# Emitting the scale of a feed-forward matrix later, and letting a reused buffer wait tile by tile

## The chip, the cores and the metric

The kernel runs on one core of a Trainium2 chip. The metric is the device time of one execution in microseconds (us); a lower one is better. Engines are called as in the profile: PE is TensorE, DVE is VectorE, ACT is ScalarE, POOL is GpSimd, SP is SyncE (which only issues transfers here).

## What is computed

A gated cross-attention block followed by a gated feed-forward block, over 16 batches of 224 tokens with 512 features. The context has 750 keys per batch, of which a mask leaves out some.

```python
x = x + tanh(g_xattn) * xattn(layernorm(x), ctx, mask, W_q, W_k, W_v, W_o, b_o)   # 8 heads of 64
x = x + tanh(g_ffn)   * ffn(layernorm(x), w1, b1, w2, b2)                        # 512 -> 2048 -> 512

def bitlinear(x, w, b):
    xq = act_quant(rmsnorm(x))          # rows to 8-bit integers and back
    scale = 1.0 / clip(mean(abs(w)), 1e-5)
    wq = clip(round(w * scale), -1, 1) / scale
    return einsum("bsd,fd->bsf", xq, wq) + b

def ffn(x, w1, b1, w2, b2):
    return bitlinear(gelu(bitlinear(x, w1, b1)), w2, b2)
```

What matters here is `scale`: it needs the mean of all absolute values of a weight matrix, so no weight can be rounded to -1, 0 or 1 before the whole matrix has been read and summed.

## The kernel before

The work goes batch by batch. The batches are sorted by how many keys the mask leaves, and only those keys are gathered: up to 192 for the first eight batches, up to 128 for the others. A sorted batch is called a slot. The loop at the end of `compact_path` runs over the 16 slots. In slot s it mixes three streams of pieces, each piece a small function with an estimated cost:

- `attention_pieces(s)`: the attention of slot s. It has empty pieces called wait, which only stand for time; `turn_probs` for the units 0 and 1 (a unit is four heads of half the tokens); the scores of units 2 and 3 (`both(2)`); `turn_probs` 2 and 3; and `weighted`, the sum over the values. `turn_probs` transposes the probabilities on PE (L1128, L1135). `scores` makes matmuls (L1074), reductions on DVE (L1088), exponentials on ACT (L1098), and a division on POOL (L1108), which `turn_probs` needs.
- `other`: what the next slots need. Norm of x (L979 to L988), gathers (L807, L880), `select(s + 3)` with six indicators on DVE (L830), then, woven together, `context_pieces(s + 1)` (transposes L905, keys L916, values L931 and L942) and `query_pieces(s + 1)` (transposes L1014, queries L1035).
- `flow`: in slot 0 the first feed-forward matrix (`weight_pieces(0)`), in slot 1 the second (`weight_pieces(1)`), from slot 2 on the output projection and the feed-forward block itself (`residual`, `project`, `normalise`, `up`, `gelu`, `down`).

`merge` takes, again and again, the next piece of the stream that is least far in terms of its own total cost; at equal shares the stream named first. After the streams come the scores of units 0 and 1 of slot s + 1. The order in which pieces are emitted is a priority: the Tile scheduler takes, for each engine, the ready instruction with the highest priority by its own model of time, and the queue that results is fixed. On the chip every engine then works through its queue in order.

A feed-forward matrix is handled in 8 chunks of 128 x 1024 values. `load_weights` reads a chunk into a `raw` tile; the chunks of the second matrix are loaded into the same 8 tiles as those of the first come free in slot 0. `sum_weights` sums absolute values (DVE L1388, ACT L1392). `scale_weights` adds up the sums (DVE L1398), sums over partitions with a matmul by ones (PE L1400) and takes reciprocals (DVE L1402 to L1411). `round_weights` multiplies and clips a chunk (DVE L1421, L1422), with three buffers for the result. `turn_weights` transposes it in eight matmuls (PE L1437 for the second matrix) and copies the result to `w2T` (an eviction, by DVE at L777 or ACT at L780). `evict` chooses the engine by two running counters of estimated work, to which other steps, `round_weights` among them, add too. The cost of a round is 0.2, of a turn 0.6, so the stream of a matrix has the total 8 x 0.8 = 6.4, and `scale_weights(1)` costs 0.

`w2T` is first read in `down` (PE L1329).

The raw tiles lie in a pool of their own, opened in `late["stage"]`. When slot 1 has been emitted, that pool is closed and the pool `rows` is opened on the memory: three `y` tiles of 4 KB per partition, three `hq` (which hold the rows of `gelu` and, in `normalise`, `fx`) and two `hqT`, 32 KB as the eight raw tiles. `residual` fetches the rows of `y` with POOL (L807) and adds the bias (L1207); `project` adds the projection (PE L1214, DVE L1217).

Of the kernel before, what the change touches and what calls it, by code (L numbers as in the profile page):

```python
# [733 lines left out]
def compact_path(ctx, tc, sh, x, context, out, late_loads, stages):  # L734
# [47 lines left out]
    def gen(shape, dtype, name):  # L782
        return ps_gen.tile(shape, dtype, tag="gen", name=name)
# [12 lines left out]
    def small(name, n=2):  # L796
        return pa.tile([P, n], F32, tag=f"s{n}", name=name, bufs=24 if n == 2 else 6)
# [73 lines left out]
    def gather(s):  # L871
        st = live[s]
        nt = 2 if CAPS[s] > P else 1
        if s:
            kept = pa.tile([P, 2, C], F32, tag="ctx", name=f"ctx_{s}", bufs=2)
        else:
            kept = early[:, 2 * D : 2 * D + 2 * C].rearrange("p (t c) -> p t c", t=2)
        for t in range(nt):
            rows = rows_of(s, t)
            nc.gpsimd.indirect_dma_start(  # L880
                out=kept[:rows, t, :],
                out_offset=None,
                in_=kctx,
                in_offset=bass.IndirectOffsetOnAxis(ap=st["keys"][:rows, t : t + 1], axis=0),
                bounds_check=B * J - 1,
                oob_is_err=False,
            )
        st["ctx"] = kept
# [163 lines left out]
    def norm_pieces(s):  # L1052
        pieces = []
        for t in tiles_of(s):
            if t % 2 == 0:
                pieces.append((0.0, lambda t=t: norm(t // 2)))
                if t // 2 + 2 < NTOK // 2:
                    pieces.append((0.0, lambda t=t: fetch(t // 2 + 2)))
        return pieces
# [138 lines left out]
    late = {}  # L1198

    def residual(i):  # L1200

        f = pairs[i] = {}
        f["y"] = y = late["rows"].tile([P, 2, D], F32, tag="y", name=f"y_{i}", bufs=3)
        for k in range(2):
            fetch_x(y[:, k, :], 2 * i + k)
        for k in range(2):
            nc.gpsimd.tensor_tensor(y[:, k, :], y[:, k, :], sh.bo, ALU.add)  # L1207
# [138 lines left out]
    def up_pieces(i):  # L1346
        p = []
        for k in range(2):
            p += [(1.8, lambda g=g, k=k: up(i, k, g)) for g in range(2)]
            p.append((0.0, lambda k=k: gelu(i, (k,))))  # L1350
        return p
# [15 lines left out]
    def load_weights(wi, c):  # L1367

        raws[wi, c] = raw = late["raw"].tile([P, W], F32, tag="raw", name=f"raw_{wi}_{c}", bufs=NPC)
        if wi == 0 and c == 0:  # L1370

            nc.scalar.copy(raw[0:1, 0:1], live[0]["ctx"][0:1, 0, 0:1])
        if wi == 0:
            return nc.sync.dma_start(
                raw.rearrange("p (a d) -> p a d", d=D),
                sh.w1_dram[c * 2 * P : (c + 1) * 2 * P, :].rearrange("(a p) d -> p a d", p=P),
            ).ins
        at = c % 2 * W
        return nc.sync.dma_start(raw, sh.w2_dram[c // 2 * P : (c // 2 + 1) * P, at : at + W]).ins

    def sum_weights(wi, c):
        if c == 0:
            weight_sums.append(pa.tile([P, NPC], F32, name=f"wsums_{wi}"))
        if c == 1:
            late["junk"] = pa.tile([P, FF], F32, tag="h", name=f"junk_{wi}", bufs=2)
        raw = raws[wi, c]
        if c % (2 + 2 * wi) == 0:
            nc.vector.tensor_reduce(  # L1388
                weight_sums[wi][:, c : c + 1], raw, AX.X, ALU.add, apply_absolute_value=True
            )  # L1390
        else:
            nc.scalar.activation(late["junk"][:, :W], raw, AF.Abs, accum_out=weight_sums[wi][:, c : c + 1])  # L1392
# [3 lines left out]
    def scale_weights(wi):  # L1396
        tot = small(f"wtot_{wi}")
        nc.vector.tensor_reduce(tot[:, 0:1], weight_sums[wi], AX.X, ALU.add)  # L1398
        pt = gen([P, 1], F32, f"wtotp_{wi}")
        nc.tensor.matmul(pt, lhsT=sh.ones, rhs=tot[:, 0:1], start=True, stop=True)  # L1400
        mean = small(f"wmean_{wi}")
        nc.vector.tensor_scalar(mean[:, 0:1], pt, 1.0 / (FF * D), 1e-5, ALU.mult, ALU.max)  # L1402
        sw = pa.tile([P, 1], F32, name=f"sw_{wi}")
        nc.vector.reciprocal(sw, mean[:, 0:1])
        isw = pa.tile([P, 1], F32, name=f"isw_{wi}")
        nc.vector.reciprocal(isw, sw)
        if wi == 0:
            nc.vector.tensor_scalar(isw, isw, 1.0 / 127.0, None, ALU.mult)
        else:

            nc.vector.tensor_scalar(isw, isw, sh.tgates[:, 1:2], 1.0 / 127.0, ALU.mult, ALU.mult)  # L1411
        weight_scale[wi] = sw
        sh.isw[wi] = isw
# [3 lines left out]
    def round_weights(wi, c):  # L1417

        raw = raws.pop((wi, c))
        quantised[wi, c] = w16 = pa.tile([P, W], BF16, tag="xq", name=f"w16_{wi}_{c}", bufs=3)  # L1420
        nc.vector.tensor_scalar(raw.bitcast(I32), raw, weight_scale[wi], None, ALU.mult)  # L1421
        nc.vector.tensor_scalar(w16, raw.bitcast(I32), 1.0, -1.0, ALU.min, ALU.max)  # L1422
        load["v"] += 1400

    def turn_weights(wi, c):
        w16 = quantised.pop((wi, c))
        pt = gen([P, 8, P], BF16, f"wp_{wi}_{c}")
        if wi == 0:

            for d in range(ND):  # L1430
                for a in range(2):
                    at = a * D + d * P
                    nc.tensor.transpose(pt[:, 2 * d + a, :], w16[:, at : at + P], ident16)
            evict(w1T[:, :, c * 2 * P : (c + 1) * 2 * P], pt.rearrange("p (d a) f -> p d (a f)", d=ND), 8 * P)
        else:
            for f in range(8):
                nc.tensor.transpose(pt[:, f, :], w16[:, f * P : (f + 1) * P], ident16)  # L1437
            f = c % 2 * 8
            evict(w2T[:, f : f + 8, c // 2 * P : (c // 2 + 1) * P], pt, 8 * P)

    def weight_pieces(wi):

        p = []
        if wi == 1:
            p += [(0.0, lambda: scale_weights(1))]
        for c in range(NPC + 2):
            if c < NPC:
                p += [(0.2, lambda c=c: round_weights(wi, c))]
                if wi == 0:
                    p += [(0.0, lambda c=c: load_weights(1, c))]  # L1450
            if c > 1:
                p += [(0.6, lambda c=c: turn_weights(wi, c - 2))]
                if wi == 0:
                    p += [(0.0, lambda c=c: sum_weights(1, c - 2))]
        return p
# [18 lines left out]
    def weave(a, b):  # L1474

        outl = []
        ia = ib = 0
        while ia < len(a) or ib < len(b):
            if ib >= len(b) or (ia < len(a) and ia * len(b) <= ib * len(a)):
                outl.append(a[ia])  # L1480
                ia += 1
            else:
                outl.append(b[ib])
                ib += 1
        return outl
# [11 lines left out]
    ctx = stages[0]  # L1497
# [40 lines left out]
    for s in range(B):  # L1538
        other = norm_pieces(s + 2) if s + 2 < B else []
        if s + 2 < B:  # L1540
            other.append((0.0, lambda s=s: gather(s + 2)))
        if s + 3 < B:
            other.append((0.0, lambda s=s: select(s + 3)))
        if s + 1 < B:
            other += weave(context_pieces(s + 1), query_pieces(s + 1))
        flow = []
        if s < 2:
            flow = weight_pieces(s)
        else:
            complete = 256 * (projected + 1) <= S * s  # L1550
            if projected == 0:
                nc.gpsimd.tensor_scalar(sh.bo, sh.bo, sh.tgates[:, 0:1], None, ALU.mult)
                nc.gpsimd.tensor_scalar(sh.b2, sh.b2, sh.tgates[:, 1:2], None, ALU.mult)
            if complete:
                flow.append((0.0, lambda i=projected: residual(i)))
            if raised < projected:
                flow += up_pieces(raised)
                raised += 1
            if complete:
                flow += project_pieces(projected)  # L1560
                projected += 1
                if lowered < raised:
                    flow += down_pieces(lowered)
                    lowered += 1
        merge(attention_pieces(s), other, flow)
        if s == 1:

            late["stage"].close()
            late["rows"] = ctx.enter_context(tc.tile_pool(name="rows", bufs=1))
        if s + 1 < B:  # L1570
            scores(s + 1, 0)
            scores(s + 1, 1)
# [45 lines left out]
```

## Time and profile before

| | us |
|---|---|
| median of 3 runs | 751.12 |
| lowest, highest | 750.07, 753.04 |
| the profiled execution | 751.76 |
| its span in the profile | 750.0 |
| PE busy | 681.3 |
| DVE busy | 499.0 |
| ACT busy | 408.0 |
| POOL busy | 394.1 |

The span runs from the first to the last instruction in the profile; the time of the execution has 1.76 us more around it. A line of the timeline gives the start and the duration in us, the engine, the source line, the operation, the tiles (written <- read), the shape and the number of instructions merged; in brackets stands the idle time before it, and what ended that. A line of the windows gives for each engine the busy time and the number of instructions, then the clock that PE was granted (1.00 is full speed) and the share and rate of the DMA engines.

### The profile page before, as it was taken

How to read it: one execution, taken by the hardware profiler on the slowest of the kernel's cores; microseconds unless marked ns; L12 is line 12 of the kernel's file. 1: busy time of each engine (PE TensorE's matmuls, PEld its weight loads, DVE VectorE, ACT ScalarE, POOL GpSimd, SP SyncE). 2: the span in 40 equal slices, each digit the busy share in tenths (PEclk: the TensorE clock that was granted, in tenths of full speed). 3: DMA queues.
4: the chain of work that ended last, by engine and by line, in shares of the span. 5: the costliest groups of instructions: out<-in, count | busy, mean ns of one | idle time of the engine just before them, and what ended most of it. 6: DMA issues, size and time to landing. Idle time of an engine off the chain costs nothing.

```text
span 750.0 us, 11362 instructions
## 1 busy us (share of the span) xinstructions
PE 681.3 (91%) x3900; PEld 434.5 (58%) x3900; DVE 499.0 (67%) x1284; ACT 408.0 (54%) x963; POOL 394.1 (53%) x541
## 2 busy tenths in 40 slices
PE   4998899999999999997999999999999999988652
PEld 3776677675656565665655665666666566443211
DVE  5586846876684684755758675588584939586860
ACT  2549645383673846635757368365565656460530
POOL 5583676463654644547366564565654453636141
PEclk9989999999999999999999999999999999999887
DMA  7794031022222312222142413123132222214250
GB/s 240 270 285 140 25 90 31 15 73 57 76 48 62 95 43 74 50 66 73 28 99 68 85 54 68 43 72 79 55 62 65 56 71 57 71 29 78 41 108 31
DMA packets 87218, 58.77 MB, mean 78 GB/s; under 512 B 75488, under 2 KB 75632, under 8 KB 87024
## 3 DMA queue, kind: packets, MB, share of 16 engines
q1 hardware_dynamic: 79024, 32.00, 18.6%
q0 software_dynamic: 8128, 25.96, 11.0%
q8 instruction: 33, 0.54, 0.3%
q14 instruction: 33, 0.27, 0.1%
HBM read 32.26 MB, written 7.34 MB: 53 GB/s over the span
## 4 chain that ended last, share of the span: by engine, by line
PE 55%; issue 13%; DVE 12%; POOL 11%; DMA 4%; ACT 3%; POOLq 0%; DVEq 0%; ACTq 0%; SPq 0%
PE qp L1035 9%; PE op L1214 9%; PE fp L1329 7%; PE hp L1284 6%; PE kp L916 5%; PE sim L1074 4%; PE vp L931 4%; POOL p L1108 2%; PE ptp L1128 2%; DVE a L1307 2%; PE av L1151 2%; DVE h L1292 2%; DMA hqT<-hq 2%; DVE hq L1310 1%; POOL y L1272 1%
## 5 line engine op out<-in xcount | busy, mean ns | idle before, releaser
L1108 POOL TENSOR_TENSOR p<-p,rec 112x768 f32<-112x768 f32 (+1 forms) x64 | 84.3, 1318 | 73.6 <-DVE rec L1107 28.5
L1329 PE MATMUL fp<-w2T,hqT 128*128 128x512 fp8e4 x448 | 104.5, 388 | 13.6 <-DMA hqT<-hq 13.6
L1284 PE MATMUL hp<-w1T,xqT 128*128 128x512 fp8e4 x448 | 107.1, 384 | 8.8 <-DVE h L1292 6.1
L1098 ACT ACTIVATE p<-p,nm 112x192 f32<-112x192 f32 (+1 forms) x256 | 106.5, 420 | 8.0 <-DVE nm L1088 7.8
L1035 PE MATMUL qp<-xnT,wq_sb 128*128 128x224 f32 x512 | 105.8, 361 | 0.6 <-ACT xnT L780 0.6
L1214 PE MATMUL op<-wo_sb,xoT 128*128 128x512 f32 x224 | 103.7, 599 | 0.0
L1035 PEld LDWEIGHTS qp<-xnT,wq_sb 128*128 128x128 f32 x512 | 97.5, 194 | 6.6 <-issue 3.3
L1292 DVE SCALAR_TENSOR_TENSOR h<-hp,c,b_bc 128x1024 f32<-128x1024 f32 x56 | 71.6, 1279 | 40.1 <-PE hp L1284 37.6
L1329 PEld LDWEIGHTS <-hqT 128*128 128x128 bf16 x448 | 43.3, 99 | 71.1 <-DMA hqT<-hq 16.7
L1088 DVE CUSTOM_DVE_ANT_0 p<-sim,mask 112x128 f32<-112x128 f32 (+1 forms) x224 | 57.9, 313 | 34.4 <-PE sim L1074 33.9
L1307 DVE TENSOR_REDUCE a<-h 128x1 f32<-128x2048 f32 x28 | 63.9, 2281 | 22.4 <-ACT h L1304 22.3
L1284 PEld LDWEIGHTS <-xqT 128*128 128x128 bf16 x448 | 43.2, 98 | 57.7 <-issue 15.4
L1333 DVE SCALAR_TENSOR_TENSOR y<-fp,c,y 128x512 f32<-128x512 f32 x28 | 20.9, 745 | 76.2 <-PE fp L1329 72.9
L1335 POOL DMA_INDIRECT out_dram<-y,token x28 | 30.9, 1104 | 75.9 <-DVE y L1333 70.4
L1315 ACT ACTIVATE h<-h 128x2048 f32<-128x2048 f32 x28 | 53.4, 1907 | 22.2 <-DVE hq L1310 14.8
L1304 ACT ACTIVATE h<-h 128x2048 f32<-128x2048 f32 x28 | 53.4, 1909 | 19.7 <-DVE k L1225 10.8
L916 PE MATMUL kp<-ctxT,wk_sb 128*128 128x192 f32 (+1 forms) x384 | 63.3, 314 | 0.0
L1214 PEld LDWEIGHTS op<-wo_sb,xoT 128*128 128x128 f32 x224 | 40.7, 190 | 38.8 <-issue 36.3
L916 PEld LDWEIGHTS kp<-ctxT,wk_sb 128*128 128x128 f32 x384 | 57.6, 198 | 6.2 <-issue 4.3
L1272 POOL TENSOR_TENSOR y<-y,b_bc 128x512 f32<-128x512 f32 x28 | 36.6, 1309 | 37.6 <-DVE fx L1253 37.4
L780 ACT COPY pT<-ptp 128x448 f32<-128x448 f32 x62 | 32.3, 536 | 42.6 <-PE ptp L1128 40.4
L1074 PE MATMUL sim<-kT,qT 64*112 64x192 f32 (+1 forms) x512 | 51.0, 313 | 1.7 <-issue 0.6
(173 smaller groups left out, 1172.4 us busy)
## 6 DMA issues: line engine op xcount, KB each, us to landing
raw<-in_L_ffn_w_dram SPq DMA_DIRECT2D x16, 512.0 KB
wq_sb<-in_L_xattn_W_q_dram SPq DMA_DIRECT2D x1, 1024.0 KB
b_bc<-in_L_ffn_b_dram SPq DMA_DIRECT2D x1, 1024.0 KB
wk_sb<-in_L_xattn_W_k_dram SPq DMA_DIRECT2D x1, 768.0 KB
wv_sb<-in_L_xattn_W_v_dram SPq DMA_DIRECT2D x1, 768.0 KB
wo_sb<-in_L_xattn_W_o_dram SPq DMA_DIRECT2D x1, 512.0 KB
wo_sb<-in_L_xattn_W_o_dram SPq DMA_DIRECT2D x2, 256.0 KB
y<-in_x_dram,token POOLq DMA_INDIRECT x28
```

What stands on the lines that cost most here:

```text
L916: nc.tensor.matmul(pk[:, p - p0, :], lhsT=sh.wk[:, c, p * P : (p + 1) * P], rhs=st["ctxT"][:, c, :cap], start=(c == 0), stop=(c == NC - 1),)
L1035: nc.tensor.matmul(pq[:, i, :], lhsT=sh.wq[:, d, (p + i) * P : (p + i + 1) * P], rhs=st["xnT"][:, d, :], start=(d == 0), stop=(d == ND - 1),)
L1074: nc.tensor.matmul(sim[:, j, i, :cap], lhsT=st["qT"][j * DH : (j + 1) * DH, p, q * TQ : (q + 1) * TQ], rhs=st["kT"][j * DH : (j + 1) * DH, ...
L1088: nc.vector.tensor_tensor_reduce(out=probs[:, h, :cap], in0=sim[:, j, i, :cap], in1=st["mask"][:, j * begin : j * begin + cap], scale=-(DH ...
L1098: nc.scalar.activation(probs[:, h, :cap], probs[:, h, :cap], AF.Exp, bias=nmax, scale=-1.0, accum_out=total[:TQ, h : h + 1],)
L1108: nc.gpsimd.tensor_tensor(probs[:, :, :cap], probs[:, :, :cap], rec[:TQ].unsqueeze(2).to_broadcast([TQ, 4, cap]), ALU.mult,)
L1214: nc.tensor.matmul(po, lhsT=xoT[:, d, at : at + P], rhs=sh.wo[:, d, :], start=(d == 0), stop=(d == ND - 1))
L1284: nc.tensor.matmul(ph[:, n, :], lhsT=f["xqT"][:, k * ND + d, :], rhs=w1T[:, d, at : at + NB], start=(d == 0), stop=(d == ND - 1),)
L1292: nc.vector.scalar_tensor_tensor(h[:, cols], ph.rearrange("t i n -> t (i n)"), f["c1", k], sh.b1[:, cols], ALU.mult, ALU.add)
L1304: nc.scalar.activation(f["h", k], f["h", k], AF.Gelu)
L1307: nc.vector.tensor_reduce(amax[:, k : k + 1], h, AX.X, ALU.max, apply_absolute_value=True)
L1329: nc.tensor.matmul(po, lhsT=f["hqT", k][:, n, :], rhs=w2T[:, n, :], start=(n == 0), stop=(n == NF - 1))
```

## The change

In `weight_pieces(1)` an empty piece of cost 3.0 is put ahead of `scale_weights(1)`. It issues nothing; it raises the total of the stream from 6.4 to 9.4 and makes `merge` turn to the other two streams until they have reached a share of 3.0 / 9.4. And the pool `rows` is opened with `reuse_waits="tile"`, as the raw pool is already: a new tile then waits for the release of the old tiles that lie under it, where otherwise each new tile waits for the whole old pool.

```diff
@@ -1442,7 +1442,7 @@
         p = []
         if wi == 1:
-            p += [(0.0, lambda: scale_weights(1))]
+            p += [(3.0, lambda: None), (0.0, lambda: scale_weights(1))]
         for c in range(NPC + 2):
             if c < NPC:
                 p += [(0.2, lambda c=c: round_weights(wi, c))]
@@ -1566,7 +1566,7 @@
         if s == 1:
 
             late["stage"].close()
-            late["rows"] = ctx.enter_context(tc.tile_pool(name="rows", bufs=1))
+            late["rows"] = ctx.enter_context(tc.tile_pool(name="rows", bufs=1, reuse_waits="tile"))
         if s + 1 < B:
             scores(s + 1, 0)
             scores(s + 1, 1)
```

## The prediction

> **What bounds the kernel now.** I read the page first: TensorE (PE) is busy for 91% of the span and no other engine passes 67%, so time is lost only where TensorE stands still or runs at a reduced clock.
>
> ```profile
> PE 681.3 (91%) x3900; PEld 434.5 (58%) x3900; DVE 499.0 (67%) x1284; ACT 408.0 (54%) x963; POOL 394.1 (53%) x541
> PEclk9989999999999999999999999999999999999887
> ```
>
> Then I cut slot 1, the stretch that the change touches (about 78 to 111 us), into windows of one microsecond. Columns: PE, weight loads, DVE, ACT, POOL busy, granted clock, DMA share, GB/s.
>
> ```profile
> 81.00:82.00 1.00, 0.08 (x2) 0.00 (x0) 1.00 (x11) 1.00 (x6) 0.50 (x1) 1.00 0.00 0
> 83.00:84.00 1.00, 0.06 (x1) 0.00 (x0) 1.00 (x8) 0.58 (x1) 0.86 (x3) 1.00 0.00 0
> 84.00:85.00 1.00, 0.00 (x0) 0.00 (x0) 1.00 (x3) 0.00 (x0) 0.89 (x2) 1.00 0.00 0
> 85.00:86.00 1.00, 0.80 (x10) 0.61 (x10) 1.00 (x3) 0.14 (x1) 1.00 (x1) 0.87 0.00 0
> 87.00:88.00 1.00, 1.00 (x5) 1.00 (x4) 1.00 (x3) 0.70 (x3) 1.00 (x1) 0.50 0.00 0
> 89.00:90.00 1.00, 1.00 (x7) 1.00 (x7) 1.00 (x4) 0.00 (x0) 1.00 (x1) 0.93 0.00 0
> ```
>
> TensorE is nearly empty from 81 to 85 while DVE is full, and afterwards its clock is halved for over three microseconds. The timeline of TensorE gives the reason:
>
> ```profile
> 79.48 1.61 PE L1074 MATMUL sim<-kT,qT 64*112 64x192 f32 x16
> 82.21 0.35 PE L1400 MATMUL wtotp<-wtot,ones 128*128 128x1 f32 x2 [1.13 <-DVE wtot L1398]
> 82.42 0.64 PE L1014 MATMUL xnp<-ident,x 128*128 128x128 f32 x4
> 85.20 0.62 PE L1437 MATMUL wp<-ident,w 128*128 128x128 bf16 x8 [2.14 <-DVE w L1422]
> 85.66 0.65 PE L905 MATMUL ctxp<-ident,ctx 128*128 128x128 f32 x2
> 87.14 3.10 PE L916 MATMUL kp<-ctxT,wk_sb 128*128 128x192 f32 x12
> ```
>
> Two of its instructions wait for DVE: the sum of the second weight matrix (L1400, 1.13 us) and the first transposes of its rounded weights (L1437, 2.14 us). Behind them stand context transposes and key projections whose inputs are there. The timeline of DVE shows why it is late: wtot comes behind the score reductions, and between it and the first rounded chunk lie four indicators of select:
>
> ```profile
> 81.91 0.15 DVE L1398 TENSOR_REDUCE wtot<-wsums 128x1 f32<-128x8 f32 x1
> 81.98 1.23 DVE L830 TENSOR_SCALAR ind<-place,upto 125x192 bf16<-125x192 bf16 x2
> 84.46 0.68 DVE L1422 TENSOR_SCALAR w<-raw 128x1024 bf16<-128x1024 int32 x1
> ```
>
> The wait ends on DVE, not on a load: wtot starts without idle time before it, and the last partial sum of ScalarE (L1392) was done at 72.3.
>
> **What the Trainium skill says.** "TensorE: Matmul & The Clock Gate", section "Step-by-step: what each phase is for": matmuls stay in program order, only weight loads are pulled ahead. The trace agrees: xnp and ctxp stand behind wtotp and wp. The same page, Part 1 ("What's actually happening"): the clock falls to half after an idle window of about 3.4 us and comes back after a busy one. Here 0.50 was granted from about 85.9 to 89.1. "SBUF — State Buffer", "Who interferes with whom": GpSimd and a DVE instruction in a two-port mode (tensor_scalar among them) lock each other out. The trace fits: two L988 took 3.94 us beside the rounding, where one has a median of 0.76.
>
> **Part one, the piece of cost 3.0.** It adds no instruction and removes none. merge always takes the stream that is least far in share of its cost. Worked through for the kernel before, this gives the order that the trace shows. There, the flow's total is 6.4: scale and rounds 0 to 2 come after the first context transposes, and t0 (transposes of chunk 0) ahead of the second, the keys and turn_probs. Now the total is 9.4, the empty piece brings the flow at once to 0.32, and scale follows only behind the context and xn transposes, both key projections, turn_probs 0 and 1 and both score units (shares 0.43, 0.385). Tile's scheduler may still fill gaps out of order, but now at lower priority.
>
> What goes: 1.13 + 2.14 = 3.27 us of waiting, and the halved clock, (1-0.87) + 3 x 0.50 + (1-0.93) = 1.70 us. Together 4.97, the ceiling.
> What comes back, first: the keys need ctxT from ScalarE, which is in exponentials until 82.85, then copies xnT (0.58) and ctxT (0.33): keys at about 83.8. TensorE has 0.60 + 0.49 + 0.60 of transposes from 81.1, hence is free at 82.8; a turn_probs of 0.58 can fill part. I put 0.5 us for it, bounded by 0 and 1.0.
> Second, the replay: keys 2.06, turn_probs 1, the second keys 2.06 and q0 3.1 bring TensorE to turn_probs 2 at about 93.5 (98.04 less 4.5). Its input comes from POOL:
>
> ```profile
> 84.56 3.94 POOL L988 TENSOR_SCALAR x<-x,ls_x,rs_x 128x512 f32<-128x512 f32 x2
> 88.68 1.82 POOL L880 DMA_INDIRECT ctx<-in_ctx_dram,keys  x1 [0.17 <-PE kp L916]
> 94.45 2.89 POOL L1108 TENSOR_TENSOR p<-p,rec 112x768 f32<-112x768 f32 x2
> 100.24 1.05 POOL L807 DMA_INDIRECT y<-in_x_dram,token  x1 [2.89 <-DVE w L1422]
> ```
>
> POOL is without a pause from 84.56 to 97.34, so p of unit 2 (ready at 95.9) has 2.1 us in hand today and would be 2.4 late. But the 3.94 falls to 1.5 if rounding no longer runs beside it: 86.1, four gathers of 1.3 end at 91.4, p of unit 2 at 92.9, of unit 3 at 94.3, against 93.5 and 94.9. It just fits; I put 0.4 us for it, bounds 0 and 2.4.
> Third, the rounds: 8 x (0.75 + 0.68) = 11.4 us of DVE work, done at 99.97 now, begin some 5 us later. DVE is busy for 2.77 of the 11 us from 100 to 111, so this cover holds them; gone, each late chunk would cost up to 1.43 us. Nobody needs w2T before L1329 at 173. By evict's counters four copies go over to DVE early in the slot and three to ScalarE late (0.2 to 0.6 us each), under other work. No DMA and nothing of SP's queue moves with the pieces.
>
> **Part two, the waits of the rows.** The pool rows lies where the raw chunks lay: 8 x 4 KB each, y on chunks 0 to 2, hq on 3 to 5, hqT on 6 and 7. Before, the first fetch of y waits for the last rounding (2.89 us above); POOL then works on six fetches (1.01 + 0.30 each) and six additions (1.27) until 116.47, with unit 0 of slot 2 behind them. Now y waits for chunks 0 to 2 only. By itself this is worth 0: y is first used by DVE at 118.82, and TensorE is busy in 11.0 of 11.0 us before 111. It is the cover of part one: with the last round at some 104 and TensorE 4 us earlier, the old wait could cost up to 4 us.
>
> **Sum.** 3.27 + 1.70 - 0.5 - 0.4 = 4.1 us. Between 111 and 190 us TensorE idles 0.2 us in 79, so the gain is handed on; later waits hang on TensorE's own results and move with it. The profiled execution took 751.76 us (span 750.0, 1.76 around it) and would take 747.7. It stands 0.64 above the median of 751.12, from which the same gain leads to 747.0.
>
> **The rivals.** (A) As above: 747.0, 745.9 to 748.3; chance 0.64. More, with all 4.97 and some of slot 2's POOL queue: about 745.5; 0.06.
> (B) The wait moves to POOL. The gathers stay slow because rounding fills the same gap; turn_probs 2 waits 2.4 us: gain 4.97 - 0.5 - 2.4 = 2.1, 749.0; 0.19. For it: POOL's unbroken run. Against: the scheduler can put values and q2 ahead.
> (C) The change doesn't do what it says: the scheduler sees idle engines and emits t0 in the same gap, or Tile keeps the wait for the whole pool. Gain at most the 1.13: about 750.5; 0.05. Against: xnp and ctxp were ready and go first now.
> (D) Slower: since y waits for three chunks only, its six fetches get ahead of p of units 2 and 3 in POOL's queue: 6 x 1.31 = 7.9 us, and they stand there until DVE has rounded. TensorE loses 7.9 - 0.6 + 1.7 of clock - 4.1 = 4.9 net: 756.0; 0.06. It decides from 4.7 us of POOL work ahead of p (four fetches). Against: y has the lowest priority and DVE is still rounding then.
>
> **How the numbers follow.** About 0.5%, 3.8 us, is what a measurement of this kernel can tell from no change. The bound for faster is 747.36: of A 0.42 lies below, with the larger gain 0.48. Same: 0.22 + 0.19 + 0.05 + 0.01 of D = 0.47; slower 0.05. The range 744.8 to 751.5 takes in A to C and the ends of the two unknown waits, and leaves out D and the tail of the larger gain.
>
> **What would show it.** Right: L1400 and the first L1437 behind the key projections, no wait of a microsecond for DVE there, clock 1.00 from 81 to 92, two L988 near 1.5 us, the first y fetch before the last L1422, L1074 of slot 2 at about 107 and not 111.3. Wrong: turn_probs of slot 1 waiting for L1108 by 2 us or more (B, D), y fetches ahead of L1108 (D), or the clock dip at another place of slot 1.

## The result and the profile after

| | before | after |
|---|---|---|
| median, side by side on one chip | 751.85 (8 runs) | 757.91 (8 runs) |
| lowest, highest | 749.70, 753.17 | 754.35, 760.04 |
| the profiled execution | 751.76 | 754.35 |
| its span | 750.0 | 752.5 |

The kernel became slower: the ratio after to before is 1.0067, with a 95% interval of 1.0043 to 1.009. In a second series the same kernel took 757.09 against 751.49, a ratio of 1.0072 (1.0048 to 1.0095). The sign of the forecast was wrong.

The page of the profile after, as the first look at the one before: TensorE is busy for 3.0 us more with the same 3900 matmuls, and DVE for 3.6 us less. More busy time for the same work points at the clock or at the order of the work, not at added work.

```profile
PE 684.3 (91%) x3900; PEld 435.2 (58%) x3900; DVE 495.4 (66%) x1285; ACT 408.1 (54%) x962; POOL 391.1 (52%) x541
PEclk9989989999999999999999999999999999999887
```

The windows of one microsecond of the kernel after (columns as in the prediction: PE, weight loads, DVE, ACT, POOL, clock, DMA share, GB/s; `...` stands for lines left out, here and below):

```profile
81.00:82.00 1.00, 1.00 (x8) 0.76 (x7) 0.84 (x5) 0.59 (x3) 0.70 (x2) 1.00 0.11 23
84.00:85.00 1.00, 1.00 (x8) 0.66 (x6) 0.73 (x3) 0.82 (x3) 0.70 (x3) 1.00 0.00 0
...
90.00:91.00 1.00, 0.00 (x0) 0.00 (x0) 0.97 (x2) 0.00 (x0) 1.00 (x2) 1.00 0.00 0
91.00:92.00 1.00, 0.00 (x0) 0.00 (x0) 1.00 (x1) 0.00 (x0) 1.00 (x1) 0.83 0.00 0
92.00:93.00 1.00, 0.00 (x0) 0.00 (x0) 1.00 (x3) 0.00 (x0) 0.20 (x1) 0.50 0.00 0
97.00:98.00 1.00, 1.00 (x4) 0.89 (x4) 1.00 (x2) 0.00 (x0) 0.00 (x0) 0.50 0.64 172
98.00:99.00 1.00, 1.00 (x6) 0.96 (x5) 0.20 (x1) 0.00 (x0) 0.00 (x0) 0.75 0.23 90
```

From 81 to 89 TensorE is full at full clock; before, it stood nearly empty up to 85 and then ran at half clock. But from 89.5 to 93.5 it is empty again, with DVE full as before, and the clock is halved for 6.8 us (91.7 to 98.5) instead of 3.4. The hole has moved by some eight microseconds and has become larger. The timeline of TensorE names its edges (start, duration, instruction; in brackets the idle time before it and what ended that):

```profile
81.31 2.22 PE L916 MATMUL kp<-ctxT,wk_sb 128*128 128x192 f32 x12
86.25 2.22 PE L916 MATMUL kp<-ctxT,wk_sb 128*128 128x192 f32 x12
88.31 0.28 PE L1400 MATMUL wtotp<-wtot,ones 128*128 128x1 f32 x2
88.51 0.98 PE L1151 MATMUL av<-pT,v 128*64 128x224 f32 x8
93.54 1.04 PE L1437 MATMUL wp<-ident,w 128*128 128x128 bf16 x8 [4.05 <-DVE w L1422]
94.37 5.29 PE L1035 MATMUL qp<-xnT,wq_sb 128*128 128x224 f32 x16
```

Both key projections do stand ahead of the sum over partitions (L1400), as forecast, and the wait of L1400 is gone. The first transposes of the rounded weights (L1437) still come right behind it: only 0.98 us of work lies between. Behind L1437 stand the queries (L1035), whose inputs are there; they wait with it and then run at half clock, 5.29 us for what took 3.25 before:

```profile
94.51 3.25 PE L1035 MATMUL qp<-xnT,wq_sb 128*128 128x224 f32 x16
```

DVE and POOL in the same microseconds of the kernel after:

```profile
89.64 0.16 DVE L1402 TENSOR_SCALAR wmean<-wtotp 128x1 f32<-128x1 f32 x1
90.11 2.64 DVE L1421 TENSOR_SCALAR raw<-raw,sw 128x1024 int32<-128x1024 f32 x1
92.68 0.20 DVE L1411 TENSOR_SCALAR isw<-isw,tgates 128x1 f32<-128x1 f32 x1
92.80 0.68 DVE L1422 TENSOR_SCALAR w<-raw 128x1024 bf16<-128x1024 int32 x1
```

```profile
87.83 1.52 POOL L988 TENSOR_SCALAR x<-x,ls_x,rs_x 128x512 f32<-128x512 f32 x2
89.32 2.88 POOL L1108 TENSOR_TENSOR p<-p,rec 112x768 f32<-112x768 f32 x2
93.75 1.33 POOL L807 DMA_INDIRECT y<-in_x_dram,token  x1 [1.55 <-DVE w L1422]
95.39 1.06 POOL L807 DMA_INDIRECT y<-in_x_dram,token  x1 [0.30 <-issue]
106.84 1.21 POOL L807 DMA_INDIRECT y<-in_x_dram,token  x1 [10.40 <-DVE w L1422]
120.52 2.89 POOL L1108 TENSOR_TENSOR p<-p,rec 112x768 f32<-112x768 f32 x2
```

The first rounding (L1421) takes 2.64 us and ends soon after POOL's two divisions (L1108) of 2.88 us: they run side by side. In the kernel before the first rounding took 0.73:

```profile
83.69 0.73 DVE L1421 TENSOR_SCALAR raw<-raw,sw 128x1024 int32<-128x1024 f32 x1
```

From the end of L1400 at 88.6 to the transposes at 93.54 it is 4.95 us: 1.05 until DVE has finished two key copies and a reciprocal that came at the same time, 0.47 of small reciprocals, 2.64 of L1421, 0.8 for L1411 and L1422. TensorE had 0.9 us of work left for it, and waits for the rest. In the kernel before, the same chain took 2.64 us (82.56 to 85.20), with 0.5 us of work in it. So TensorE's work inside the chain has hardly changed; the chain has become 2.3 us longer, and 1.9 of that is the slow rounding.

**Where the time is lost.** Lining the traces up at the reciprocals of the softmax (L1107), the kernel after is 0.72 us ahead at the first mark of slot 1 and 2.39 us behind at the first of slot 2. So 3.1 us are lost in slot 1. The offset is handed on: it is 2.4 to 2.6 at nearly all marks up to slot 7, shrinks to 1.3 at the last one (672 us), and is 2.5 at the end of the span; a stretch of half clock at 678 to 682, which the profile before does not have, costs 1.4 us there. Between the first L1107 of slot 1 and the third of slot 3 TensorE issues the same 611 matmuls in both kernels; it is empty for 4.44 us against 3.66 (+0.78) and busy for 88.19 against 85.86 (+2.33). The busy part by lines, time in which two matmuls overlap counted once: queries +2.0 and transposes L1437 +0.4 (half clock), keys -0.6 and xn -0.35 (full clock now), scores L1074 +1.0 for the same 86 matmuls, which are now issued in smaller runs between other work; that the smaller runs cost this time was not tested by itself.

The medians differ by 6 us, the profiles by 2.6. The rest goes with the granted clock of whole runs: three runs of the kernel after at a mean clock of 0.971 to 0.972 took 754.4 to 755.1, five at 0.959 to 0.965 took 757.3 to 760.0; of the kernel before, the 31 runs of all series at 0.971 took 749.6 to 755.0, with a median of 752.4. At the same clock the difference is about 2.4 us, near that of the profiles. Stretches of 3.4 us at half clock, up to 1.7 us each, lie in other places from one profile to the next, also of the same kernel: a second profile of the kernel after (span 755.4) has the same wait of 4.05 us, and more half clock at 207 and after 678. Why the kernel after has more of them in the median is open.

### The profile page after: what moved, and what is told of

It reads as the page before. It is cut to its first block, busy times and chain, and to the rows that moved or that the text cites. A ratio compares the mean times of both kernels' runs of the same rounds, so it can differ in the third digit from the quotient of the medians.

```text
span 752.5 us, 11358 instructions
## 1 busy us (share of the span) xinstructions
PE 684.3 (91%) x3900; PEld 435.2 (58%) x3900; DVE 495.4 (66%) x1285; ACT 408.1 (54%) x962; POOL 391.1 (52%) x541
## 4 chain that ended last, share of the span: by engine, by line
PE 55%; issue 14%; DVE 12%; POOL 12%; DMA 4%; ACT 3%; POOLq 0%; ACTq 0%; DVEq 0%; SPq 0%
PE qp L1035 9%; PE op L1214 9%; PE fp L1329 8%; PE hp L1284 6%; PE kp L916 5%; PE sim L1074 4%; PE vp L931 4%; POOL p L1108 3%; PE ptp L1128 2%; DVE a L1307 2%; PE av L1151 2%; DVE h L1292 2%; POOL y L807 2%; DMA hqT<-hq 2%; POOL y L1207 2%
## 5 line engine op out<-in xcount | busy, mean ns | idle before, releaser
L1108 POOL TENSOR_TENSOR p<-p,rec 112x768 f32<-112x768 f32 (+1 forms) x64 | 84.0, 1314 | 66.1 <-DVE rec L1107 27.0
L1035 PE MATMUL qp<-xnT,wq_sb 128*128 128x224 f32 x512 | 107.2, 364 | 0.6 <-ACT xnT L780 0.6
L1035 PEld LDWEIGHTS qp<-xnT,wq_sb 128*128 128x128 f32 x512 | 98.8, 197 | 6.7 <-issue 3.3
L1074 PE MATMUL sim<-kT,qT 64*112 64x192 f32 (+1 forms) x512 | 52.3, 315 | 1.0 <-DVE nm L1088 0.6
```

The source lines that it names most:

```text
L1035: nc.tensor.matmul(pq[:, i, :], lhsT=sh.wq[:, d, (p + i) * P : (p + i + 1) * P], rhs=st["xnT"][:, d, :], start=(d == 0), stop=(d == ND - 1),)
L1074: nc.tensor.matmul(sim[:, j, i, :cap], lhsT=st["qT"][j * DH : (j + 1) * DH, p, q * TQ : (q + 1) * TQ], rhs=st["kT"][j * DH : (j + 1) * DH, ...
L1108: nc.gpsimd.tensor_tensor(probs[:, :, :cap], probs[:, :, :cap], rec[:TQ].unsqueeze(2).to_broadcast([TQ, 4, cap]), ALU.mult,)
```

## The experiments

The theory from this profile (Q in the expectations): **the loss is a matter of distance in TensorE's queue.** Here the transposes of chunk 0 can start about 5 us after L1400; what lies between the two counts, not how late L1400 comes. The extra piece stands ahead of the scale and so moved both together. On top of the wait comes the clock. Rivals: that part two brought the loss (rows of y or POOL's order), that the rounds simply come too late, that the collision of DVE and POOL is the cause by itself.

This table is for all that follows: time that TensorE is empty and busy from the first L1107 of slot 1 to the third of slot 3, from one profile each; then the times, all in us.

| kernel | empty | busy | median | ratio to before (95%) |
|---|---|---|---|---|
| before | 3.66 | 85.86 | 751.5 to 752.3 | 1 |
| part two alone | 3.54 | 85.72 | 753.85 | 1.0017 (0.9999 to 1.0035) |
| part one alone | 7.45 | 89.45 | 759.37 | 1.0092 (1.0061 to 1.0123) |
| both: the change | 4.44 | 88.19 | 757.91 | 1.0067 (1.0043 to 1.009) |
| piece behind the scale | 2.58 | 84.72 | 749.72 | 0.9975 (0.9956 to 0.9994) |
| further piece ahead of the first turn | 1.10 | 86.07 | 749.28 | 0.9963 (0.9946 to 0.9979) |
| the same without part two | 4.61 | 88.54 | 756.98 | 1.0077 (1.0057 to 1.0098) |
| 4.5 instead of 3.0 | 2.73 | 87.23 | 752.66 | 1.0013 (0.9999 to 1.0027) |
| divisions on ACT | 2.41 | 87.55 | 753.51 | 1.0014 (1.0 to 1.0029) |
| first rounding on ACT | 5.08 | 87.92 | 754.89 | 1.0051 (1.0034 to 1.0067) |
| 8 useless matmuls | 0.26 | 92.47 | 757.6 | 1.0077 (1.0058 to 1.0095) |
| 4 useless matmuls | 1.68 | 89.21 | 753.46 | 1.0012 (0.999 to 1.0035) |
| further piece, and divisions on ACT | 2.01 | 86.32 | 754.88 | 1.0023 (1.0007 to 1.004) |

**Part two alone.**

```diff
-            p += [(3.0, lambda: None), (0.0, lambda: scale_weights(1))]
+            p += [(0.0, lambda: scale_weights(1))]
```

> Only the second part of the change: the pool rows waits tile by tile, the scale stays where it was. Theory Q (the whole loss is a wait of TensorE for the first rounded chunk, which the moved scale brings): TensorE's order in slot 1 is that of before, so the time is that of before within 1 us. Rival Y (the loss comes from the y fetches, which stand in POOL's queue and wait there for single chunks): slower by 2 to 5 us.

Measured: 753.85 against 752.2, no difference that can be told. TensorE's two waits are those of before, 1.13 and 2.15 us. So part two by itself is worth nothing that can be told, and does no harm that can be told.

**Part one alone.**

```diff
-            late["rows"] = ctx.enter_context(tc.tile_pool(name="rows", bufs=1, reuse_waits="tile"))
+            late["rows"] = ctx.enter_context(tc.tile_pool(name="rows", bufs=1))
```

> Only the first part: the empty piece of 3.0, the pool rows waits as a whole. Theory Q: TensorE waits about 4 us ahead of the first L1437 of the second matrix and its clock is halved afterwards, as in the changed kernel; slower than before by 3 to 6 us. Rival Y: within 1 us of before, no such loss without the new waits of the rows.

Measured: 759.37. The timeline of TensorE has the wait of slot 1 again and a second one in slot 2, for POOL, whose first fetch of y starts only at 108.56, after 15.04 us of idle time:

```profile
94.86 1.03 PE L1437 MATMUL wp<-ident,w 128*128 128x128 bf16 x8 [4.07 <-DVE w L1422]
...
126.25 0.32 PE L1128 MATMUL ptp<-ident,p 112*128 112x112 f32 x1 [3.22 <-POOL p L1108]
```

So the loss is part one's. That part two takes something off it is seen in the wait of slot 2, which the change does not have; the two ratios, 1.0092 and 1.0067, have intervals that overlap.

**The piece behind the scale instead of ahead of it.** The scale keeps its early place, only rounds and turns are emitted later.

```diff
-            p += [(3.0, lambda: None), (0.0, lambda: scale_weights(1))]
+            p += [(0.0, lambda: scale_weights(1)), (3.0, lambda: None)]
```

> Both parts, but the empty piece stands behind the scale and ahead of the rounds: the sum over partitions (L1400) keeps its old early place on TensorE, the first transposes of rounded weights come behind the second key projection. Theory Q: about 7 us of work (transposes, two key projections, turn_probs) lie between L1400 and the first L1437, so the wait of 2.14 goes and no half clock follows; the wait of about 1.1 for wtot may stay: faster than before by 2.5 to 4.5 us. A rival that says that late rounding itself costs (late chunks, crowded end of the slot): slower than before by 2 us or more, as the changed kernel.

Measured: 749.72, faster than before, though by less than the 2.5 to 4.5 us expected. The timeline of TensorE, then a line of DVE:

```profile
83.75 0.35 PE L1400 MATMUL wtotp<-wtot,ones 128*128 128x1 f32 x2 [1.12 <-DVE wtot L1398]
...
91.09 0.61 PE L1437 MATMUL wp<-ident,w 128*128 128x128 bf16 x8
91.54 3.25 PE L1035 MATMUL qp<-xnT,wq_sb 128*128 128x224 f32 x16
...
97.53 0.60 PE L1128 MATMUL ptp<-ident,p 112*128 112x112 f32 x4 [1.14 <-POOL p L1108]
```

```profile
85.23 0.73 DVE L1421 TENSOR_SCALAR raw<-raw,sw 128x1024 int32<-128x1024 f32 x1
```

L1437 stands at the same place of the queue as in the change, behind both key projections and ahead of the queries, yet does not wait: L1400 ran seven microseconds ahead of it. No clock is lost in slot 1. That is the distance, with the transposes as late as in the change. The rounds themselves were not late: DVE did the first at 85.23, five microseconds before the change did. So this run cannot tell distance from late rounds; the piece of 4.5, below, can.

**A further empty piece between the scale and the first turn**, on top of the change:

```diff
             if c > 1:
+                if wi == 1 and c == 2:
+                    p += [(1.5, lambda: None)]
                 p += [(0.6, lambda c=c: turn_weights(wi, c - 2))]
```

> The changed kernel with one more empty piece of cost 1.5 ahead of the first transposes of the second matrix; scale and rounds are emitted late as in the change. On TensorE L1400 then stands ahead of the second key projection, and the queries (16 of L1035) come ahead of the first L1437: some 6 us of work between the two. Theory Q: the wait of 4 us and the halved clock go; faster than before by 3 to 5 us, faster than the changed kernel by 6 to 10. Rival (late rounding itself costs): no better than the changed kernel.

Measured: 749.28, the lowest median here (that of the piece behind the scale is as good within the noise): 0.37% faster than before, and about 1.0% faster than the change. The profile is of an execution of 754.87, the slowest of the 17, at a clock of 0.969 where the median run had 0.976; its slots 1 and 2 ran at full clock. The timeline of TensorE, then a line of DVE:

```profile
85.80 0.29 PE L1400 MATMUL wtotp<-wtot,ones 128*128 128x1 f32 x2
...
86.86 2.22 PE L916 MATMUL kp<-ctxT,wk_sb 128*128 128x192 f32 x12
88.91 3.19 PE L1035 MATMUL qp<-xnT,wq_sb 128*128 128x224 f32 x16
91.94 1.06 PE L1437 MATMUL wp<-ident,w 128*128 128x128 bf16 x16
```

```profile
86.77 0.73 DVE L1421 TENSOR_SCALAR raw<-raw,sw 128x1024 int32<-128x1024 f32 x1
```

Now 5.9 us lie between L1400 and L1437, keys and queries among them, and neither waits. The piece also raised the stream's total to 10.9 and so brought L1400 forward. With that the first rounding no longer met POOL's divisions, which start at 90.73 here, and chunk 0 was ready 2.1 us after L1400 instead of 4.95. So distance and a shorter chain came together in this kernel. The gain of the table is less than the 2.56 us of empty time saved plus the clock: the scores, in smaller runs, cost 0.9 us more of TensorE's time than before and the sums over values (L1151) 0.5.

**The same without part two.**

```diff
-            late["rows"] = ctx.enter_context(tc.tile_pool(name="rows", bufs=1, reuse_waits="tile"))
+            late["rows"] = ctx.enter_context(tc.tile_pool(name="rows", bufs=1))
```

> The better variant turn_later with the second part of the change undone: the pool rows waits as a whole. If the prediction's part two is right, the tile by tile wait covers a loss once TensorE is ahead: the y fetches then start only after the last L1422 (about 107 us), POOL is in them and their additions until about 120, and the first turn_probs of slot 2 waits 2 to 4 us for POOL; slower than turn_later by 2 to 5 us. Rival: the second part is worth nothing, the same time as turn_later within 1 us.

Measured: 756.98. A line of TensorE's timeline in slot 2:

```profile
122.61 0.45 PE L1128 MATMUL ptp<-ident,p 112*128 112x112 f32 x1 [3.76 <-POOL p L1108]
```

The clock is halved for 6.8 us from 121.8 on. Lined up with the kernel that has part two, it is 8.1 us later from the third mark of slot 2 on, of which 2.2 were there before slot 1. So part two is a cover that late rounds need, worth here 4 us of wait and about 2 of clock.

**A longer piece, 4.5 instead of 3.0.**

```diff
-            p += [(3.0, lambda: None), (0.0, lambda: scale_weights(1))]
+            p += [(4.5, lambda: None), (0.0, lambda: scale_weights(1))]
```

> The changed kernel with an empty piece of 4.5 in place of 3.0: L1400 stays behind the second key projection, but the queries (3.1 us) come ahead of the first L1437. Theory Q: of the 5.0 us from L1400 to the first L1437 3.1 are covered by the queries, so the wait falls to 1 to 2 us and the clock is not halved; faster than the changed kernel by 4 to 7 us, 0 to 3 us faster than before. Rival (the later the rounds, the worse): slower than the changed kernel.

Measured: 752.66, better than the change by some 5 us, but no better than before, where 0 to 3 us had been expected. The timeline of TensorE, then a line of DVE:

```profile
89.06 0.28 PE L1400 MATMUL wtotp<-wtot,ones 128*128 128x1 f32 x2
89.19 3.27 PE L1035 MATMUL qp<-xnT,wq_sb 128*128 128x224 f32 x16
94.29 0.62 PE L1437 MATMUL wp<-ident,w 128*128 128x128 bf16 x8 [1.82 <-DVE w L1422]
```

```profile
90.86 2.65 DVE L1421 TENSOR_SCALAR raw<-raw,sw 128x1024 int32<-128x1024 f32 x1
```

The queries came between L1400 and L1437. They cover 3.1 us of the chain, and the wait is 1.82: together 4.95, the same sum as in the change (0.9 + 4.05). L1400 and the rounding come 0.75 us later than in the change, and the rounding is as slow; yet the wait is less than half. This is the run that separates distance from lateness. The clock was still halved once, from 95.6 to 99; that was not expected.

**Divisions of units 2 and 3 of slot 1 on ACT**, in the change:

```diff
+        if s == 1 and n > 1:
+            for h in range(4):
+                nc.scalar.activation(probs[:, h, :cap], probs[:, h, :cap], AF.Copy, scale=rec[:TQ, h : h + 1])
+        else:
             nc.gpsimd.tensor_tensor(
             ...
```

> The changed kernel with the divisions of units 2 and 3 of slot 1 on ScalarE (eight instructions of one head each) and not on POOL; the order of TensorE and the place of the first rounding in DVE's queue are those of the changed kernel. It takes away what ran on POOL beside the first rounding. If that collision lengthens the wait, the first L1421 of the second matrix (here two to five lines further down) takes about 0.75 us and not 2.64, the wait of 4.05 us falls to about 2.2, and with a shorter gap less of the clock is halved: faster than the changed kernel by 2 to 5 us. If the collision is no part of it, the time is that of the changed kernel.

Measured: 753.51, some 4 us better than the change and not to be told from before. The lines of DVE and TensorE (numbers are 4 higher in this kernel, L1425 is the rounding and L1441 the transposes):

```profile
90.78 0.73 DVE L1425 TENSOR_SCALAR raw<-raw,sw 128x1024 int32<-128x1024 f32 x1
```

```profile
92.29 0.99 PE L1441 MATMUL wp<-ident,w 128*128 128x128 bf16 x8 [2.14 <-DVE w L1426]
```

With POOL out of the way the rounding takes 0.73 us again, and the wait shrinks by 1.91, which is what the rounding lost. So the collision is 1.9 of the 4.05 us. What remains, 2.14, is distance: the chain without the collision, 3.0 us, less the 0.9 of work in it. It is as long as the wait of the kernel before, and it is followed by one stretch of half clock (92.4 to 95.8), as there. So two questions have two answers: the distance is why the wait did not go, and the collision, with the second stretch of half clock, is why the change is slower than before.

**First rounding on ACT**, in the change; a miss.

```diff
-        nc.vector.tensor_scalar(raw.bitcast(I32), raw, weight_scale[wi], None, ALU.mult)
+        if wi == 1 and c == 0:
+            nc.scalar.activation(raw.bitcast(I32), raw, AF.Copy, scale=weight_scale[wi])
+        else:
+            nc.vector.tensor_scalar(raw.bitcast(I32), raw, weight_scale[wi], None, ALU.mult)
```

> The changed kernel with the multiplication of chunk 0 of the second matrix on ScalarE, which is idle then, and not on DVE; the order of TensorE is that of the changed kernel. It takes away the collision of that instruction with the divisions on POOL (2.64 us on DVE where 0.75 is usual). If the collision is part of the cause, the wait of 4.05 us falls to about 2.5 and the time by 1.5 to 3.5 us against the changed kernel. If only the place in the queue counts and DVE would have been late anyway, the time is that of the changed kernel.

Measured: 754.89, lower than the change, but with an interval that overlaps its own; and a wait of 4.70, not less. DVE put the rounding of the next chunk into the gap, and that one met the divisions (numbers are 3 higher here):

```profile
89.62 2.64 DVE L1424 TENSOR_SCALAR raw<-raw,sw 128x1024 int32<-128x1024 f32 x1
```

Chunk 0, done on ACT at 90.7, then waited for its second step behind it. The run says nothing on the theory, except that DVE kept to the order of its queue too.

**Useless matmuls in the gap**: eight, then four f32 matmuls of 128 x 128 by 128 x 512, whose result nobody reads, right behind L1400.

```diff
-        nc.tensor.matmul(pt, lhsT=sh.ones, rhs=tot[:, 0:1], start=True, stop=True)
+        summed = nc.tensor.matmul(pt, lhsT=sh.ones, rhs=tot[:, 0:1], start=True, stop=True)
+        if wi == 1:
+            warm = gen([P, D], F32, "warm")
+            with tc.issue_after(summed.ins):
+                for _ in range(8):
+                    nc.tensor.matmul(warm, lhsT=ident, rhs=sh.wq[:, 0, :], start=True, stop=True)
```

> The changed kernel with eight extra matmuls of 128x512 (f32, results unused) on TensorE between L1400 and the first L1437 of the second matrix: some 3.4 us of useless work that fills the wait and nothing else; all work of the kernel stays. If the halved clock after the gap is a part of the loss of its own, it goes (two stretches, 3.4 us) while the first rounded chunk comes no earlier: faster than the changed kernel by 2 to 4 us. If only the wait counts, the time is that of the changed kernel or a little more.

Measured: 757.6, as slow as the change. I had sized them wrongly, from the transposes: the eight took 7.11 us, so L1437 came at 95.43 instead of 93.54. Even so the work behind the queries began earlier than in the change (98.96 against 99.49), since the clock stayed at 1.00; but 0.98 us of sums over values (L1151), which the change had done in the gap, was then still to do. With four:

> The changed kernel with four instead of eight useless f32 matmuls (128x128 by 128x512, the result is read by nobody) on TensorE right behind the sum over partitions, L1400. Eight took 7.11 us, so four take about 3.6 us, less than the 4.05 us that TensorE waits there. Theory Q (queue distance plus halved clock): the wait ahead of the first L1437 shrinks to 0.5 to 1 us, the first L1437 stays at about 93.5, the clock stays 1.00 from 91 to 98, and the queries' 16 matmuls take about 3.25 us, so the end of slot 1 comes 2 to 3.5 us earlier than in the changed kernel although 3.6 us of work were added: about 3 us faster than the changed kernel. Rival (the wait itself costs, the clock nothing): no difference from the changed kernel, 757 to 758. Rival (the loss is contention of engines with each other, and a fuller TensorE makes it worse): slower.

Measured: 753.46, some 4 us better than the change with 3.7 us of work more; the intervals of the two ratios do not overlap. The timeline of TensorE (numbers are 5 higher here) and the window that was at 0.50 in the change:

```profile
88.93 3.68 PE L1405 MATMUL warm<-wq_sb,ident 128*128 128x512 f32 x8
94.03 0.62 PE L1442 MATMUL wp<-ident,w 128*128 128x128 bf16 x8 [1.42 <-DVE w L1427]
94.49 3.25 PE L1035 MATMUL qp<-xnT,wq_sb 128*128 128x224 f32 x16
```

```profile
97.00:98.00 1.00, 1.00 (x12) 0.91 (x12) 1.00 (x2) 0.23 (x1) 0.00 (x0) 1.00 0.52 201
```

The transposes begin half a microsecond later than in the change and the work behind the queries 1.9 us earlier (97.57 against 99.49). That is the clock's share by itself, some 2.4 us of slot 1, and it is taken off with work that computes nothing. From it goes the L1151 that is still to do here as well: from the first L1107 of slot 1 to the third of slot 3 it is 90.89 us against 92.63.

**Both remedies together**, the further piece and the divisions on ACT.

> Both remedies together: the changed kernel with a further empty piece of 1.5 before the first turn of the second matrix, and with the divisions of units 2 and 3 of slot 1 on ScalarE (eight activations, a Copy with the scale rec) in place of two tensor_tensor of POOL. Theory Q: the empty piece has already put the queries between L1400 and the first L1437, so that no wait of a microsecond for the rounds is left, and the faster rounds have nothing more to give there: within 1.5 us of the kernel with the empty piece alone, 748 to 750. Rival (DVE and POOL standing in each other's way is a loss of its own, whatever TensorE has between): the 1.9 us that the divisions' move saved in the other kernel come again, 747 to 747.5.

Measured: 754.88, neither. No wait of a microsecond is left in slot 1, but a new one appears in slot 2, and the kernel is 1.1 us behind the one with the further piece from there on:

```profile
118.03 0.29 PE L1132 MATMUL ptp<-ident,p 112*128 112x112 f32 x1 [1.78 <-DVE y L1221]
```

```profile
112.05 4.97 DVE L830 TENSOR_SCALAR ind<-place,upto 125x192 bf16<-125x192 bf16 x6
115.68 1.27 POOL L1211 TENSOR_TENSOR y<-y,bo_bc 128x512 f32<-128x512 f32 x1
```

DVE works through six indicators of select (L830) until 117 there; a reciprocal and L1221 (the projection's addition, L1217 before) come behind them. The six take 4.97 us beside POOL's work on p and y, 3.20 with the further piece alone and 1.34 in the change: the 1.77 more are as long as the new wait. So the moved divisions changed the order elsewhere, and DVE and POOL met at another place. The rest of the 5.6 us between the medians goes with a lower clock of whole runs (median 0.969 against 0.976); why it is lower is open. I had expected at most 1.5. Nothing was gained; but as the two engines did not keep apart, this run does not rule the rival out.

**The change once more** served to tell scatter from cause:

> The changed kernel once more, for a second profile and more times. Theory Q: the same wait of about 4 us ahead of the first L1437 of the second matrix; slower than before by 3 to 6 us. Where the whole time differs from the first profile by more than 1 us, the extra should stand as stretches of about 3.4 us at half clock, each worth 1.7 us, and not as new waits.

Measured: 757.09, told of above.

## Why the prediction was wrong

The step that failed is "What goes": of 1.13 + 2.14 us of waiting only the 1.13 went. The 2.14 became 4.05, and the 1.70 of half clock, which was to go with it, became two stretches, 2.5 us by the windows. The prediction had let the wait for chunk 0 vanish without working out where its transposes would stand, and had put the price of moving the rounds at nothing.

- **What bounds the kernel.** Right. The two waits and the halved clock are real and can be removed: the piece behind the scale and the further piece, which take L1437 away from L1400, make it 0.25% and 0.37% faster.
- **"Together 4.97, the ceiling."** Not reached. The half clock that followed the old wait was worth 1.70 by the windows (it began at 85.74, not 85.9), but the new order also cost: 0.9 to 1.0 us for scores in smaller runs, in the change and with the further piece. The best kernel gained 2.9 us in the median.
- **"What comes back, first": 0.5 us for ctxT.** Came to nothing: both key projections start without a wait (81.31, 86.25).
- **"Second, the replay"; here the wait was lost from sight.** It took TensorE from the second keys over q0 (the queries) to turn_probs 2 and left the transposes of chunk 0 out. The prediction's own numbers place them: when the scale is emitted, the other streams stand at 0.43 (the one with the queries next) and 0.385 (attention). The three rounds ahead of the first turn bring the flow from 3.0 to 3.6 of 9.4, which is 0.383, below both; so the turn is the next piece emitted, ahead of the queries. Before, the distance from scale to turn was 0.6 of 6.4, 0.094 of the stream; after it is 0.6 of 9.4, 0.064. A piece ahead of both puts nothing between them. The same arithmetic orders the other kernels: with the piece behind the scale the turn is at 3.6 of 9.4 again, and stands ahead of the queries; with 4.5 it is at 5.1 of 10.9, 0.468, and with the further piece at the same 0.468, and in both the queries, at 0.43, come first. The traces show these orders.
- **"Third, the rounds", priced at 0.** Wrong for chunk 0, and by more than the 1.43 us per chunk named as its worst: DVE's slack from 100 to 111 covers the late chunks, but the first one is needed at once. The wait for it was 4.05 us. Of this, 1.9 us are the collision with L1108. The prediction had quoted the Trainium skill, "SBUF — State Buffer", "Who interferes with whom", for L988, and found that this collision goes: it does, 1.52 us. It did not ask whom the moved rounds would meet: the trace shows the same again, for L1421 (2.64 us) beside L1108.
- **The clock.** The Trainium skill, "TensorE: Matmul & The Clock Gate", Part 1, speaks of an idle window of about 3.4 us. Read as the length of a wait, that lets too much pass: waits of 2.14 us (divisions on ACT) and 1.82 us (4.5) were followed by 3.4 us of half clock, with TensorE busy for 1.3 and 1.6 us in the 3.4 us ahead of it. The kernel before had shown the same, with a wait of 2.14 and 1.3 us busy. In the change the wait of 4.05 gave two such stretches. The prediction had named "the clock dip at another place of slot 1" as a sign of being wrong, and it came.
- **POOL, 0.4 us put.** Right for L988, which falls to 1.52 us, and no turn_probs of slot 1 waits for L1108, which runs at 89.32. But that is in part luck: two gathers went ahead at 80.18 and 81.54, and TensorE reached turn_probs 2 only at 100.38 instead of 93.5. With the further piece, where it got there at 92.83, the wait for POOL in slot 1 was 0.18.
- **Part two.** Worth 0 by itself and up to 4 us as a cover: both measured (1.0017; waits of 3.22 and 3.76 us without it). "Now y waits for chunks 0 to 2 only" did not hold: the third fetch waits 10.40 us for a round that ends only after 106; which chunk lies under it, and why, was not followed. It still just fits: p of slot 2 starts at 120.52 and TensorE takes it at 122.04 without a wait.
- **Handed on.** Right for the most part, with the other sign: of the 2.39 us of slot 2, 1.3 are left at the last mark.
- **The rivals.** (C) had the mechanism, "emits t0 in the same gap", but bought it as an accident of the scheduler and with the scale early, so it could only gain less. (D) forecast 756.0, and that it lies near the result is luck: its cause did not come, since the y fetches stand behind L1108. The missing rival is (C) with the scale late as well: a wait of the same kind, longer by the collision, and two half-clock stretches.

## What to carry to other kernels

When a producer chain across engines is moved, look at the distance between its first and its last instruction in each in-order queue, not only at how late it comes: a delay ahead of the chain moves both ends, and work put between them hides it. Place the moved steps on every engine's timeline and ask whom each meets there, since that sets how long the chain takes at its new place. Price a TensorE wait of about two microseconds or more with the half clock that may follow it.

## What was not expected of the hardware

- Half-clock stretches come in units of 3.4 us (1.7 us lost if TensorE is busy throughout). In slots 1 and 2 they followed waits of 4.05, 3.22, 2.14 and 1.82 us, and did not follow waits of 1.42, 1.14 and 1.78 us.
- One DVE tensor_scalar of 128 x 1024 took 2.64 us instead of 0.73 beside two tensor_tensor of POOL (2.88 us): it got through only near their end, while they took no longer than the two in slot 2 (2.89). With the further piece and the divisions on ACT six small ones (L830) took 4.97 us beside POOL, 1.34 in the change.
- Useless matmuls on TensorE in a hole made a kernel faster than the same kernel with the hole: 753.46 against 757.91.
